# Cutting one long score product in two around a short one, in six of the twelve phases of an attention kernel

## The chip, the cores and the metric

The kernel runs on one core of one Trainium2 chip. The metric is the device time of one execution in microseconds. The kernel before took 1794.05 us (median of three runs, 1793.87 to 1794.19).

## What is computed

The input x has 32 images of 256 channels and 32 x 32 pixels, float32. With S = 1024 pixels (tokens), 8 heads of 32 channels, and a mask that lets a token see only tokens before it:

```python
xf = groupnorm(x, 32 groups).reshape(B, C, S)
q  = einsum('oc,bcs->bos', q_w,  xf) + q_b
kv = einsum('oc,bcs->bos', kv_w, xf) + kv_b        # k: first 256 rows, v: last 256
scores = einsum('bhqd,bhkd->bhqk', q, k) / sqrt(32)
scores = where(mask == 0, -10000, scores)
attn   = where(mask == 0, 0, softmax(scores))
out    = einsum('bhqk,bhkd->bhqd', attn, v)
return x + out.reshape(B, C, H, W)
```

All of it is float32. A float32 product on TensorE shows in the trace as two passes: two weight loads and two matmul records for each product of the program.

## The kernel before

**Batch, group, phase.** One image (a batch, b) is two groups of four heads (g), and each group is six phases (i = 0 to 5), so a batch is 12 phases and the whole run 384. The list VISITS (L583) says which blocks of the lower triangle of scores a phase computes. A phase has "longs" (up to 512 queries against one block of 128 keys) and "shorts": either a rectangle of 256 queries, or, in the phases 0, 1, 3 and 4, which PAIRS (L592) lists, the two blocks on the diagonal. `pair` (L291) lays such a pair out in 192 columns; for each half of the keys it takes one product of 128 columns and one of 64.

**Heads as row strips.** Head j has its 32 channels in the partitions 32j to 32j+31. One score product (`score`, L307) therefore uses 32 rows of TensorE's array, and with 64 keys 64 of its columns. Two heads with two halves of keys make four products of one size, which the program issues one after another. This document calls such four products a **wave**. The waves of heads 2 and 3 ("high") use the lower half of the array's rows, those of heads 0 and 1 ("low") the other half.

**PSUM.** A phase owns three PSUM tiles of two banks each: one for the longs of heads 0 and 1, one for the longs of heads 2 and 3, and one for the shorts of all four (L356). In the last of them a low head and a high head share a bank. The low shorts therefore wait on a semaphore, `bank_free`, which the last short of each high head and key half raises (L372 to L379).

**The order in a phase** is written out in `scores` (L348) and is the program's order on TensorE; the schedule is manual (L660), so nothing reorders it at build time. For a phase with one long and a pair (1, 3 and 4) it is:

1. high shorts: a wave of 128 columns, then one of 64
2. low long: a wave of 512
3. high long: a wave of 512
4. behind `bank_free`: low shorts, a wave of 128, then one of 64

Phase 0 has a pair and two longs (384 and 128 columns). There the list `begin` (L363) has two entries, and L364 to L365 take the high shorts in reverse (the wave of 64 first) with the 128-column low long between them. The function `scores_of` (L316) does that by its arguments `between` and `order`.

**After the scores**, ScalarE takes three exponentials from the three PSUM tiles (L391 to L397), GpSimd masks the diagonal blocks (L339), TensorE does one projection unit of the next batch (`pp` or `ppv`, L169), and then multiplies the exponentials of the phase before with the values (`acc`, L422). VectorE adds up keys (L440). DMAs fold the sums and move x, the inverses and the output; some of SP's DMAs are held back by `with_scores` (L511) until `bank_free` has reached a phase's count.

Of the kernel before, what the change touches and what calls it, by code (L numbers as in the profile page):

```python
# [26 lines left out]
HALFBANK = HALF // 2  # L27
# [5 lines left out]
def tile_norm_attention_residual(  # L33
# [65 lines left out]
    def unshifted():  # L99
# [207 lines left out]
        def score(b, g, bank, j, op):  # L307

            c, kb, first, width, cols = op
            rows = slice(HD * j, HD * (j + 1))  # L310
            return nc.tensor.matmul(  # L311
                bank[c : c + KEYS, cols], lhsT=live["k", b, g][rows, kb * P + c : kb * P + c + KEYS],
                rhs=live["q", b, g][rows, first : first + width], start=True, stop=True, skip_group_check=True,
            )

        def scores_of(b, g, bank_of, heads, entries, between=lambda: None, order=slice(None)):  # L316

            done = {}
            for _, _, halves in entries:
                for k, n in enumerate(list(range(max(map(len, halves))))[order]):  # L320
                    if k:
                        between()
                    for j in heads:
                        for c, ops in enumerate(halves):
                            if n < len(ops):
                                done.setdefault((j, c), []).append(score(b, g, bank_of(j), j, ops[n]))
            return done

        def mask(b, g, raw, j):


            hf, place = j // 2, (2 * j % 4) * P
            if ("e", b, g, "D", hf) not in live:
                live["e", b, g, "D", hf] = epool.tile(
                    [P, 4, HALF], F32, tag=("e0", "e")[hf], bufs=4, name=f"diagonal_{b}_{g}_{hf}"
                )
            square = live["e", b, g, "D", hf]
            for s in range(2):
                nc.gpsimd.affine_select(  # L339
                    out=square[:, :, place + s * P : place + (s + 1) * P],  # L340
                    in_=raw[:, :, (1 - s) * KEYS : (3 - s) * KEYS],
                    pattern=[[0, 4], [(1, -1)[s], P]], compare_op=ALU.is_gt, fill=0.0, base=0,
                    channel_multiplier=(-1, 1)[s],
                )
            if j == 0:
                nc.gpsimd.memset(square[0:1, :, 0:1], 1.0)

        def scores(b, v):  # L348


            g, i = divmod(v, len(VISITS))
            longs, shorts = VISITS[i]
            name = f"{b}_{g}_{i}"
            e = epool.tile([P, 4, HALF], F32, tag="e0" if i == TOTAL else "e", bufs=4, name=f"e_{name}")
            eh = epool.tile([P, 4, HALFBANK], F32, tag="eh", bufs=3, name=f"eh_{name}")
            pairs = [ps_s.tile([P, 2, HALF], F32, tag="sT", name=f"sT_{name}_{a}") for a in range(3)]  # L356
            short = pairs[2].rearrange("p bank (n q) -> p bank n q", n=2)
            short_of = lambda heads, *how: scores_of(
                b, g, lambda j: short[:, j % 2, j // 2, :], heads, shorts, *how
            )  # L360
            long_of = lambda heads, n: scores_of(b, g, lambda j: pairs[j // 2][:, j % 2, :], heads, longs[n : n + 1])
            rest = [lambda: long_of((2, 3), 1)] if len(longs) > 1 else []
            begin = [lambda n=n: long_of((0, 1), n) for n in range(len(longs) - 1, -1, -1)]  # L363
            if i in PAIRS and len(longs) > 1:  # L364
                first = short_of((2, 3), begin.pop(0), slice(None, None, -1))  # L365
            else:
                first = short_of((2, 3))
            for f in begin:
                f()
            long_of((2, 3), 0)  # L370

            ends = [made[-1] for made in first.values()]  # L372
            first = [ins for made in first.values() for ins in made]
            for ins in ends:
                ins.then_inc(bank_free, 1)
            for ins in first:
                tc.no_tile_sem_insts.add(ins.ins.name)
            live["free"] = live.get("free", 0) + len(ends)
            wait = nc.tensor.wait_ge(bank_free, live["free"])  # L379
            for ins in first:  # L380
                tc.declare_no_dep(wait.ins, ins.ins, reason="the semaphore orders them")
            made = short_of((0, 1), *rest if i in PAIRS else ())
            if i not in PAIRS:
                for f in rest:
                    f()
            for made in made.values():
                for lo in made:
                    for ins in first:
                        tc.declare_no_dep(lo.ins, ins.ins, reason="the semaphore orders them")
            wide, narrow = (max(at + width for at, width, _ in entries) for entries in (longs, shorts))  # L390
            for a in range(3):  # L391
                if a == 2:
                    exp = nc.scalar.activation(  # L393
                        eh.rearrange("p (n bank) q -> p bank n q", n=2)[:, :, :, :narrow], short[:, :, :, :narrow], AF.Exp
                    )
                else:
                    nc.scalar.activation(e[:, 2 * a : 2 * a + 2, :wide], pairs[a][:, :, :wide], AF.Exp)  # L397

            for ins in first:
                tc.add_to_no_dep_group(f"first_{name}", ins.ins)  # L400
                tc.add_to_no_dep_group("first", ins.ins)
            tc.declare_no_dep(exp.ins, group=f"first_{name}", reason="through the last two products")
            tc.declare_fence(exp.ins, group=f"first_{name}")
            live["e", b, g, "L", i], live["e", b, g, "H", i] = e, eh
            if i in PAIRS:
                mask(b, g, eh, PAIRS[i])

# [182 lines left out]
        ]  # L590
        N, TOTAL = NG * len(VISITS), 2
        PAIRS = {0: 0, 1: 1, 3: 3, 4: 2}  # L592

        PRODUCTS = [
            (0, [
# [36 lines left out]
        at, between, after = {}, {}, {}  # L632
# [27 lines left out]
        with tc.manual_schedule(engines={ENG.PE, ENG.Activation, ENG.DVE, ENG.Pool, ENG.SP}):  # L660
# [45 lines left out]
            for b in range(B):  # L706
                first, last = b * N, b == B - 1
# [3 lines left out]
                if b >= 2:  # L711
                    for n in range(NG * NH):
                        cols = slice(n % NH * HALF, (n % NH + 1) * HALF)
# [36 lines left out]
            for i in range(B * N + 1):  # L750
                if i < B * N:
                    scores(*divmod(i, N))
                for f in at.pop(i, ()):
                    f()
                b, v = divmod(i - 1, N)
                if i == B * N:

                    sums(3, SUMMED[v], False)
                if i:
                    values(b, v)  # L760
                    for f in between.pop(i, ()):
                        f()
                    if b < B - 1 or v not in SUMMED or v == 1:
                        add_keys(b, v)
                if i in (B * N - 2, B * N - 1):

                    sums(3, SUMMED[v])
                for f in after.pop(i, ()):
                    f()
# [9 lines left out]
    def shifted():  # L779


        with ExitStack() as inner:
# [34 lines left out]
            with tc.For_i(0, B, 1) as b:  # L817
# [93 lines left out]
                )  # L911

    inside = unshifted()
    ALL = 3 * P * ROW
    held = nc.values_load(
# [29 lines left out]
```

## Time and profile before

| what | value |
|---|---|
| median of three runs | 1794.05 us |
| the profiled execution's own time | 1793.44 us |
| its span in the trace | 1791.7 us |
| TensorE busy (matmuls) | 1784.4 us |
| VectorE / ScalarE / GpSimd busy | 1673.4 / 1456.4 / 881.3 us |
| granted TensorE clock | 0.999 |
| one batch, from a phase 0 to the next batch's phase 0 (from the second batch on) | 55.09 us |

How to read it: "PE" is TensorE's matmuls and "PEld" its weight loads. Matmul records overlap, because four row or column strips work side by side and because a record's end is modelled. A busy share near 100% therefore doesn't say that the array is full, and a mean duration of one record isn't the time by which it moves the end. What counts is where one record starts after another. All starts that are told below in ns are counted from the first weight load of the phase that they belong to.

### The profile page before, as it was taken

What the parts mean: (1) busy time and instruction counts of PE and PEld (TensorE: products, weight loads), DVE (VectorE), ACT (ScalarE), POOL (GpSimd) and SP (SyncE); (2) the same over time, 40 slices, a digit from 0 to 9 for tenths busy, and PEclk for the clock granted to TensorE, in tenths of its full rate; (3) what the DMA queues carried; (4) which work ended last, traced back from release to release, by engine and by line L of the source; (5) the groups of instructions that cost most, each with busy time, mean ns of one, the idle gap of its engine ahead of it and who ended that gap; (6) DMA issues with size and microseconds to landing.
All of it is one profiled execution on the core that took longest, in us unless ns stands there. A gap on an engine that the chain in (4) does not pass through costs nothing.

```text
span 1791.7 us, 81825 instructions
## 1 busy us (share of the span) xinstructions
PE 1784.4 (100%) x37036; PEld 948.2 (53%) x37036; DVE 1673.4 (93%) x1826; ACT 1456.4 (81%) x1990; POOL 881.3 (49%) x903
## 2 busy tenths in 40 slices
PE   9999999999999999999999999999999999999998
PEld 5555555555555555555555555555555555555554
DVE  4689999999999999999999999999999999999998
ACT  6888878888788888788887888878888878888785
POOL 2345544554545555445554455454555544555452
PEclk9999999999999999999999999999999999999999
DMA  2566766767667766766676676767776667666664
GB/s 70 105 115 137 134 134 129 147 135 143 127 126 149 140 138 134 135 139 138 139 135 131 129 150 132 145 125 128 149 141 135 136 134 138 139 139 137 132 107 106
DMA packets 86818, 236.77 MB, mean 132 GB/s; under 512 B 21312, under 2 KB 22336, under 8 KB 70592
## 3 DMA queue, kind: packets, MB, share of 16 engines
q0 software_dynamic: 15872, 97.53, 40.1%
q1 hardware_dynamic: 70448, 133.89, 25.5%
q8 instruction: 290, 4.75, 1.1%
q14 instruction: 64, 0.52, 0.1%
q10 hardware_dynamic: 144, 0.07, 0.0%
HBM read 66.85 MB, written 34.57 MB: 57 GB/s over the span
## 4 chain that ended last, share of the span: by engine, by line
PE 99%; ACT 0%; DVE 0%; issue 0%; POOL 0%; POOLq 0%
PE sT L311 31%; PE acc L422 28%; PE pp L169 26%; PE ppv L169 13%; PE pd L474 1%; PE busy L155 0%; ACT e L397 0%; PE pv L169 0%; PE pm L169 0%; PE wt L148 0%; DVE rb_last L547 0%; ACT eh L393 0%; DVE rb_last L534 0%; DVE turned L531 0%; DVE acc L544 0%
## 5 line engine op out<-in xcount | busy, mean ns | idle before, releaser
L339 POOL TENSOR_SCALAR_AFFINE_SELECT diagonal<-eh 128x512 f32<-128x512 f32 x512 | 632.5, 1256 | 841.5 <-ACT eh L393 840.9
L397 ACT ACTIVATE e<-sT 128x1024 f32<-128x1024 f32 x768 | 744.4, 1022 | 250.3 <-PE sT L311 225.9
L440 DVE TENSOR_TENSOR e<-e,e 128x1024 f32<-128x1024 f32 x314 | 574.2, 1829 | 24.5 <-ACT v L275 3.2
L311 PE MATMUL sT<-q,k 32*64 32x128 f32 (+2 forms) x18432 | 578.4, 372 | 0.1
L311 PEld LDWEIGHTS sT<-q,k 32*64 32x64 f32 x18432 | 394.8, 131 | 188.4 <-PE sT L311 69.6
L169 PE MATMUL pp<-xn,wT 128*32 128x512 f32 x4096 | 492.2, 598 | 0.0
L422 PE MATMUL acc<-e,v 128*32 128x512 f32 (+3 forms) x4608 | 401.0, 450 | 0.0
L393 ACT ACTIVATE eh<-sT 128x768 f32<-128x768 f32 (+1 forms) x384 | 341.7, 890 | 0.0
L422 PEld LDWEIGHTS acc<-e,v 128*32 128x32 f32 x4608 | 149.2, 110 | 261.5 <-issue 238.9
L169 PE MATMUL ppv<-wT,xn 128*32 128x256 f32 x4096 | 247.5, 382 | 0.0
L440 DVE TENSOR_TENSOR diagonal<-diagonal,e 128x1536 f32<-128x1536 f32 x126 | 195.0, 1548 | 16.8 <-PE acc L422 9.2
L169 PEld LDWEIGHTS pp<-xn,wT 128*32 128x32 f32 x4096 | 107.0, 109 | 195.7 <-issue 163.7
L440 DVE TENSOR_TENSOR e<-e,eh 128x1024 f32<-128x1024 f32 x126 | 164.2, 1303 | 6.5
L422 PEld LDWEIGHTS acc<-diagonal,v 128*32 128x32 f32 x4096 | 121.1, 110 | 87.6 <-issue 76.0
L440 DVE TENSOR_TENSOR e<-e,diagonal 128x2048 f32<-128x2048 f32 x63 | 144.2, 2289 | 19.8 <-POOL diagonal L339 19.8
L169 PEld LDWEIGHTS ppv<-wT,xn 128*32 128x32 f32 x4096 | 120.1, 109 | 79.7 <-issue 7.0
L422 PE MATMUL acc<-diagonal,v 128*32 128x128 f32 x4096 | 158.7, 273 | 0.0
L244 ACT ACTIVATE xn<-x,shift,rstd 128x256 f32<-128x256 f32 x248 | 136.8, 608 | 0.6 <-POOL shift L229 0.6
L544 DVE TENSOR_TENSOR num<-num,rb 128x512 f32<-128x512 f32 x124 | 123.3, 994 | 0.2 <-DMA rb<-inverses 0.2
L453 POOL DMA_DIRECT2D e<-e x124 | 103.3, 833 | 38.2 <-issue 38.2
L547 DVE SCALAR_TENSOR_TENSOR rb<-num,v_bias_col,x 128x256 f32<-128x256 f32 x248 | 117.5, 515 | 4.4
L453 POOL DMA_DIRECT2D diagonal<-diagonal x124 | 104.1, 839 | 4.8 <-issue 4.8
(84 smaller groups left out, 984.4 us busy)
## 6 DMA issues: line engine op xcount, KB each, us to landing
x<-in_x_dram SPq DMA_DIRECT2D x124, 256.0 KB, 3.7
diagonal<-diagonal POOLq DMA_DIRECT2D x62, 512.0 KB, 5.4
e<-e POOLq DMA_DIRECT2D x62, 512.0 KB, 5.9
rb<-inverses SPq DMA_DIRECT2D x124, 256.0 KB, 3.9
out_dram<-rb SPq DMA_DIRECT2D x124, 256.0 KB, 4.9
diagonal<-diagonal POOLq DMA_DIRECT2D x62, 256.0 KB, 4.6
folded<-diagonal SPq DMA_DIRECT2D x62, 256.0 KB, 5.1
e<-e POOLq DMA_DIRECT2D x62, 256.0 KB, 5.0
```

The lines of the kernel that those rows point to most:

```text
L169: nc.tensor.matmul(out[part], lhsT=lhsT[:, part], rhs=rhs, start=start, stop=stop, skip_group_check=True)
L244: nc.scalar.activation(to, of, AF.Identity, bias=live["shift", b][:, g : g + 1], scale=rstd)
L311: return nc.tensor.matmul(bank[c : c + KEYS, cols], lhsT=live["k", b, g][rows, kb * P + c : kb * P + c + KEYS], rhs=live["q", b, g][rows, ...
L339: nc.gpsimd.affine_select(out=square[:, :, place + s * P : place + (s + 1) * P], in_=raw[:, :, (1 - s) * KEYS : (3 - s) * KEYS], pattern=[ ...
L393: exp = nc.scalar.activation(eh.rearrange("p (n bank) q -> p bank n q", n=2)[:, :, :, :narrow], short[:, :, :, :narrow], AF.Exp)
L397: nc.scalar.activation(e[:, 2 * a : 2 * a + 2, :wide], pairs[a][:, :, :wide], AF.Exp)
L422: nc.tensor.matmul(acc[HD * j : HD * (j + 1), of], lhsT=live["v", b][:, kb, h * HD : (h + 1) * HD], rhs=e[:, j, :], start=first, stop=last ...
L440: nc.vector.tensor_add(to, to, tile_of(b, g, at))
L453: nc.gpsimd.dma_start(out=total[:rows], in_=total[rows : 2 * rows], accum_op=ALU.add)
L474: nc.tensor.matmul(pd[HD * j : HD * (j + 1), of], lhsT=pick, rhs=e[:, j, :], start=start, stop=stop, skip_group_check=True,)
L544: nc.vector.tensor_mul(num, num, rb)
L547: nc.vector.scalar_tensor_tensor(blocks(rb, s), blocks(num, s, (start + s) % 2 == 1), v_bias_col[:, g : g + 1], blocks(xt[:, g, cols], s), ...
```

## The change

In the phases 1, 3 and 4 of both groups (six of a batch's twelve) the low long, one wave of 512 columns, becomes two waves of 256 columns each, written to the two halves of the same banks. They are put around the high short of 128 columns, and the high short of 64 columns now comes first. All other phases stay as they are, and no other engine gets, loses or moves an instruction.

```diff
+        def part_of(b, g, bank, entry, n):
+
+            at, _, halves = entry
+            start = n * HALFBANK
+            for j in (0, 1):
+                for ((c, kb, first, _, cols),) in halves:
+                    score(b, g, bank[:, j, :], j, (
+                        c, kb, first + start, HALFBANK, slice(cols.start + start, cols.start + start + HALFBANK)
+                    ))
...
-            if i in PAIRS and len(longs) > 1:
+            if i in SPLIT:
+                begin = [lambda n=n: part_of(b, g, pairs[0], longs[0], n) for n in range(2)]
+            if i in PAIRS and len(begin) > 1:
                 first = short_of((2, 3), begin.pop(0), slice(None, None, -1))
             else:
                 first = short_of((2, 3))
...
         PAIRS = {0: 0, 1: 1, 3: 3, 4: 2}
+        SPLIT = 1, 3, 4
```

The order of these phases, before and after (H: heads 2 and 3, L: heads 0 and 1, with the columns of the wave):

```
before:  H128  H64   L512  H512  | bank_free |  L128  L64
after:   H64   L256  H128  L256  H512  | bank_free |  L128  L64
```

## Prediction

> **What bounds the kernel now.** I read the busy times and the chain of waits first, then the list of TensorE's waits, then groups by shape, then single phases.
>
> ```profile
> PE 1784.4 (100%) x37036; PEld 948.2 (53%) x37036; DVE 1673.4 (93%) x1826; ACT 1456.4 (81%) x1990; POOL 881.3 (49%) x903
> ...
> PE 99%; ACT 0%; DVE 0%; issue 0%; POOL 0%; POOLq 0%
> PE sT L311 31%; PE acc L422 28%; PE pp L169 26%; PE ppv L169 13%; PE pd L474 1%; PE busy L155 0%; ACT e L397 0%; PE pv L169 0%; PE pm L169 0%; PE wt L148 0%; DVE rb_last L547 0%; ACT eh L393 0%; DVE rb_last L534 0%; DVE turned L531 0%; DVE acc L544 0%
> ```
>
> The chain that ends last is TensorE's own stream, 99% of it, and the scores (sT) are 31%. VectorE's 93% does not set the end. The phase starts of one batch and the next lie 55.09 us apart, within 2 ns from the second batch on, so a saving inside a phase repeats 32 times.
>
> The groups by shape give the waves concerned:
>
> ```profile
> L311 PE MATMUL sT<-q,k 32*64 32x512 f32 x4096 | 359.4, 600 | 0.1
> L311 PE MATMUL sT<-q,k 32*64 32x128 f32 x6144 | 284.2, 278 | 0.0
> L311 PE MATMUL sT<-q,k 32*64 32x64 f32 x4096 | 155.8, 220 | 0.0
> ```
>
> The means (600 ns) include latency. What moves the end is the start-to-start distance of two passes on one row strip, read record by record: 429 ns for 512 columns, 216 for 256, 109 for 128, 56 for 64. The next view is the busy table over a phase 1, the one phase 4 with a longer time, and a phase 0; the first column is the phase from its first weight load to the first load of the work behind it.
>
> ```profile
> 904.77:906.18 1.40, 1.40 (x52) 1.06 (x48) 1.26 (x3) 0.78 (x2) 1.40 (x2) 1.00 0.10 18
> ...
> 918.55:919.97 1.41, 1.41 (x60) 1.07 (x48) 1.38 (x3) 0.37 (x2) 1.41 (x2) 1.00 0.00 0
> ...
> 927.79:929.21 1.42, 1.42 (x68) 1.16 (x64) 1.42 (x1) 1.25 (x3) 0.89 (x1) 1.00 0.51 188
> ```
>
> The phases 1, 3, 7, 9, 10 of a batch (7, 9 and 10 are 1, 3 and 4 of the second group) take 1403.6 ns, phase 4 takes 1410.9, phase 0 1419.3, all within a few ns in all batches.
>
> **Where those 1403.6 ns go.** Each half of the array has 704 columns to stream: two passes of 512, 128 and 64, or 2 x (429 + 109 + 56) = 1188 ns. High loads at 0, streams from 52 (as its second pass at 162 shows), and its 512 starts at 385 and 817: it is done at about 817 + 20 + 429. Low loads only at 53, streams from 106, and is never held up after that: 512 at 106 and 535, 128 at 964 and 1074, 64 at 1183 and 1239. The last of its four starts at 1259, and the next work's load comes 145 ns later, at 1404. So **low sets the end, and what it lost is the start**: 53 ns. Products are handed out 6.7 ns apart in program order; two high waves (8 x 6.7 = 53) stand ahead of it. In phase 0, 2 and 5 only one high wave stands ahead, and low loads at 27.
>
> **Two rules of the Trainium skill.** "TensorE: Matmul & The Clock Gate", in Part 3, "The mechanism", says that matmuls start in strict program order. The trace differs: in phase 5 the low wave's second pass starts at 188 and the earlier-issued high wave's second pass at 268. Order holds on a row strip, not across strips; I go by the trace, and so cutting low's long cannot hold high back by order alone. The same page (its table at the top) gives a queue of 64 entries with a partial reorder window. This the trace supports, sharply. In phase 0 (H64 L128 H128 L384 H384) the first of the H384 products loads at 280, when its strip is free, but the 2nd to 4th load at 357, 373 and 390. A product is four entries, so the 18th product of a phase is 17 x 4 = 68 entries behind the first. The first product's second pass starts at 108 and its record takes 217, so it ends at 325, and 31 ns later the 18th loads. The 30th product (L64) loads at 1133, and the 13th (L384) ends at 620 + 481 = 1101: 31 ns again. So a product is let in when the one 17 places ahead is finished, and then one per 17 ns. The delay shows in these ends, 17 ns apart, of the second pass of H384:
>
> ```profile
> 928.09 0.92 PE L311 MATMUL sT<-q,k 32*64 32x384 f32 x14
> 928.09 0.93 PE L311 MATMUL sT<-q,k 32*64 32x384 f32 x15
> 928.09 0.95 PE L311 MATMUL sT<-q,k 32*64 32x384 f32 x16
> ```
>
> I go by this rule for the forecast.
>
> **The change, part by part.**
>
> 1. *Four more products in each of 192 phases* (768 in all, 1536 weight loads and as many passes). Low streams four passes of 216 (864) in place of two of 429 (858): +6 ns a phase on low. The loads themselves lie under the other passes: each new pass of 216 ns hides a load that has to lead by 52.
> 2. *64 first, low second.* Low loads at 27, not 53: -26 ns. Its passes: 256 at 79, 295, 511, 727; 128 at 943 and 1052; 64 at 1161 and 1217, last of four 1237; next load 145 later, **1382**.
> 3. *The semaphore.* It is now raised by the 128, whose second pass starts at 278 to 298 and ends 267 later: 565. Before, the 64's ended at 347 + 217 = 564. The low shorts behind it load at 730 in phase 0 with the same end, and are due at 943. SP's held DMAs are released at the same time. No cost.
> 4. *What is queued behind:* H512 is now products 17 to 20. The first three waves stand as in phase 0 as far as timing goes (64 first, 128 third), so its loads come at 280, 357, 373, 390. A load leads its stream by 52, so the fourth one streams from 442, not 20 behind the first (387 + 20 = 407). Its second pass starts at 442 + 429 = 871. From the last second pass to the next load: 145 ns for 64 columns (56 + 89), 302 for 256 (216 + 86), so about 429 + 85 = 514 for 512. Next load at **1385 to 1386**.
>
> High is now the later by some 4 ns, and sets the end: **1386**. Gain 1403.6 - 1386 = 17.6 ns in five phases of a batch. In phase 4 of the first group the fourth product of L512, the 12th of the phase, loads 6 ns late (17 places behind the `acc` work, across the small `pm` product), which costs 7 ns to the end; the 12th product is now an H128, due only at 111, so this goes too: 1410.9 - 1386 = 24.9. A batch: 5 x 17.6 + 24.9 = 112.9 ns; 32 batches: 3.61 us. In the last batch two of the phases (2.05 and 2.63 us long) wait for ScalarE inside, and I give them nothing: -0.035. **Sum -3.58 us.** Against the profiled execution (1793.44, span 1791.7) that is a span of 1788.1; the median stands 0.6 us above that execution, so 1794.05 - 3.58 = **1790.5 us**.
>
> *ScalarE:* its first exponential waits for the low long: before, last pass at 555 + 588 = 1143; after, 747 + 374 = 1121, 22 ns earlier against a phase 18 shorter, so TensorE's later waits for exponentials keep their distance. The second exponential needs H512, at 871 + 587 = 1458 and not 1424, but the first one takes 1022, so it isn't due before 2140. VectorE has 3.9 us of idle time in a batch (7% of 55), and nothing is taken from it. All other engines' programs are the same in order and number.
>
> **Rivals.**
>
> - *No late loads (H512 comes all at once).* If the queue rule doesn't hold in this order, low ends the phase at 1382: 21.6 x 5 + 28.9 = 137 ns a batch, -4.35 us, **1789.7**. For it: the rule is read from one phase kind. Against: two exact hits of 31 ns. Chance 0.12.
> - *The gain is lost again.* Either the wave order brings low no earlier load, or H512 comes a little later than in phase 0; at 18 ns later the phase is back at 1404: **1794**. Chance 0.11 with all cases between this and the forecast.
> - *Slower: H512 is held behind the second L256.* It stands behind it in program order. If it could be let in only when that wave starts (511 in place of 280), it would stream from 563 to 583, its second pass would start at 1012, and the phase would end at 1526: +122 ns in 192 phases, +23.5 us, **1817.6**. It decides from a fourth load at 408, against 390. For it: everything behind a full queue waits in order. Against: in phase 0 H384 loads at 280 behind an L384 that starts at 298. Any lesser delay of this kind that costs over 3.6 us (19 ns a phase) is in this case's chance, 0.10.
> - The change does what it says: the instruction order of TensorE shows exactly the four waves moved, so no chance is kept for that rival.
>
> **How the numbers follow.** Forecast 0.67 at 1790.5 (its own width 1790.0 to 1791.1: 3 ns on each phase, mostly from the 514). A measurement of this kernel tells about 0.2% (3.59 us) from no change, and the forecast stands on that line. So its 0.67 splits in about equal parts; with the first rival faster is 0.45, with the second rival same is 0.45, slower 0.10. The range runs from just under the first rival, 1789.5, into the second, 1793.2, which leaves out some 0.17.
>
> **What would show it.** In the new trace: low's first load at 27; L256 at 79 (effective), 295, 511, 727; loads of H512 at 280, 357, 373, 390; last second pass of H512 at 871; phases of 1386 ns; a batch of 54.98 us; 768 more products. It is wrong if H512's loads come later than 390, if low's second L256 doesn't start at 511, or if the time between phases grows.

## The result and the profile after

The changed kernel takes 1802.22 us (median of 6 runs, 1801.38 to 1803.64) and the kernel before, on the same chip, 1794.01 us (1793.7 to 1794.19). The ratio is 1.0046, with a 95% interval of 1.0033 to 1.0059: slower by about 8.2 us, where 3.6 us less than before were forecast. The time is outside the range, and on the other side of the kernel before. (Of all the executions in this document one, of e7, had a granted clock of 0.65 and took 2580 us; it is left out of the ratios.)

Three lines of the page, after:

```profile
PE 1790.5 (99%) x38572; PEld 956.5 (53%) x38572; DVE 1668.6 (93%) x1826; ACT 1455.6 (81%) x1990; POOL 867.6 (48%) x903
...
q8 instruction: 302, 4.95, 1.1%
...
PE 99%; ACT 0%; issue 0%; DVE 0%; DMA 0%; POOLq 0%; POOL 0%; SPq 0%; ACTq 0%
```

The span is 1800.6 us and this execution's own time 1802.27. TensorE still sets the end (99%), and it has the 1536 matmuls more that were announced. Two things are new. "issue", a wait for nothing that the profile shows, has moved up in the chain. And queue 8, which carries the instructions themselves, moved 302 blocks. Before it moved fewer:

```profile
q8 instruction: 290, 4.75, 1.1%
```

The columns are packets, megabytes and the share of the DMA engines. 4.95 MB in 302 packets are 16 KB each, which fits 256 entries of 64 bytes, if a product is four entries (two loads, two matmuls): the 768 new products are then 3072 entries, and these are the 12 blocks more.

TensorE's own waits (total, times, longest) name the second surprise:

```profile
PE sT L311 <- issue: 1.4, 4, 0.6
PE pp L169 <- ACT e L409: 0.9, 1, 0.9
```

Neither line was there before. They count only the time in which no matmul record is open, and records overlap and end late, so the loss itself is larger (it is measured below). Of the groups by shape, the 512s lost 1536 of their 4096 records, and the 256s gained 3072:

```profile
L311 PE MATMUL sT<-q,k 32*64 32x256 f32 x5120 | 373.5, 387 | 0.3 <-ACT e L409 0.3
...
L311 PE MATMUL sT<-q,k 32*64 32x512 f32 x2560 | 302.1, 598 | 0.0
L311 PE MATMUL sT<-q,k 32*64 32x128 f32 x6144 | 282.2, 276 | 1.4 <-issue 1.4
```

The busy table over a phase 3, a phase 4 and the longest phase 10 (the same columns as in the prediction):

```profile
918.23:919.64 1.41, 1.41 (x60) 1.09 (x56) 1.38 (x4) 1.11 (x3) 0.00 (x0) 1.00 0.91 180
923.26:924.68 1.41, 1.41 (x68) 1.09 (x56) 1.38 (x3) 0.40 (x2) 1.41 (x2) 1.00 0.04 12
119.90:122.40 2.50, 1.94 (x60) 1.26 (x56) 2.39 (x3) 1.60 (x3) 1.24 (x2) 1.00 0.02 1
```

An ordinary changed phase takes 1411 to 1412 ns, forecast 1386. Some changed phases take far longer: this phase 10 takes 2.50 us, and TensorE has a record open for 1.94 of them.

**Where the 8 us are.** I took the times from one phase start to the next for the batches 1 to 30, the 10th percentile of each of the 12 steps as its clean time, and everything over 100 ns above as a **gap**. The sum of the 12 clean steps, the **clean batch**, is 55.130 us, before 55.087: +0.043 x 30 = 1.3 us. There are 13 gaps, in the phases 1, 7 and 10, of 7.3 us together. The sum, 8.6 us, is the difference of the two traces in these batches (8.61). Against the forecast (-0.113 us a batch, or 55.09 to 54.98) that makes two faults: 25 ns too much in every changed phase, and gaps.

**Fault one: the low shorts load late.** Up to the low shorts all starts of the waves stand where the prediction has them, to 1 ns: low loads at 27, the later L256 passes start at 295, 511, 727, H512 loads at 280, 357, 373, 390, and the last of its second passes starts at 872. The exception is the low shorts behind `bank_free`. First the weight loads of a phase 3 before (it starts at 913.53), then after (918.23); the brackets hold the idle time and who ended it:

```profile
914.26 0.50 PEld L311 LDWEIGHTS sT<-q,k 32*64 32x64 f32 x12 [0.19 <-PE sT L311]
```

```profile
919.15 0.29 PEld L311 LDWEIGHTS sT<-q,k 32*64 32x64 f32 x9 [0.26 <-PE sT L311]
```

They load at 727 before and at 920 after. The stream follows 53 later, at 973, and is due at 943: 30 ns late, and 1382 + 30 = 1412 is the phase. The signalling 128-column wave itself ends at 565, as forecast. But ahead of it in program order stands L256, on another row strip, and its last record ends at 315 + 374 = 689. The trace also records each raise of `bank_free`. Before, the four stand at 557, 600, 642 and 685; after, at 750, 792, 835 and 877. In both, the load follows the fourth by 42 to 43 ns. So it is the signal that is late, by 193 ns, and its first raise comes only after the end of L256. These times show one thing more: the four raises follow one another 42.5 ns apart, and these three distances are 128 of the 165 ns that the prediction's numbers have between the end of the signalling wave and the load.

**Fault two: TensorE has no instructions.** The longest phase 10 (it starts at 119.90), as the timeline shows it:

```profile
120.29 1.07 PE L311 MATMUL sT<-q,k 32*64 32x512 f32 x17
...
121.09 1.02 ACT L409 ACTIVATE e<-sT 128x1024 f32<-128x1024 f32 x1 [0.90 <-PE sT L311]
...
121.92 0.33 PE L311 MATMUL sT<-q,k 32*64 32x128 f32 x4 [0.56 <-issue]
121.92 0.20 PEld L311 LDWEIGHTS sT<-q,k 32*64 32x64 f32 x7 [0.91 <-issue]
```

The last raise of `bank_free` came 0.877 us into this phase, at 120.78, and yet TensorE starts nothing from 120.99 to 121.92. The transfer log has one 16 KB block on queue 8 that ended 0.63 us after this phase's start, at 120.53: 1.4 us ahead of the gap's end.

Two countings tie the gaps to the blocks. The first counts TensorE's entries in the trace from the first one on, in the order of their starts. The five longest pauses between two starts in the batches 1 to 30 (0.96 to 0.56 us) come just after 4801, 15041, 31169, 53441 and 62401 entries, and each of these numbers is 193 more than a multiple of 256. The pauses stand at one place of a block, though at different places of the program. The second compares times. Call *margin* the time from the end of a block's transfer to the moment when TensorE gets to the block's first entry. Before, the margin was 1.60 us at the least, and there are no gaps. After, the six longest pauses at a block's start (0.96 to 0.32 us) have margins of 0.46 to 1.06 us, and margin and pause add up to 1.36 to 1.47 us each time (the next, 1.34 and 0.28, fits less well). So in this trace **a block is usable about 1.4 us after its last byte, and TensorE pauses when the margin is less**. How much of a pause becomes a gap depends on what is still running: in e5 below, eight margins of 0.77 to 1.05 us delay TensorE's entries by 0.24 to 0.51 us, but cost a batch at most 0.12 us.

Where a transfer is called for can only be fitted: in this trace every transfer starts 1 to 5.6 us after the entry that stands 320 entries ahead of its block, and takes about 1 us (0.9 to 1.8).

The wait of `pp` that the profile puts down to the exponential `e` is one of these gaps (a pause of 0.96 us, margin 0.50, in phase 1 of batch 6). First the lines of that place, ScalarE's and TensorE's, then those of batch 7, without a gap:

```profile
356.71 1.94 ACT L409 ACTIVATE e<-sT 128x1024 f32<-128x1024 f32 x2 [0.46 <-PE sT L311]
```

```profile
357.89 1.06 PE L169 MATMUL pp<-xn,wT 128*32 128x512 f32 x8 [0.89 <-ACT e L409]
```

```profile
413.08 1.94 ACT L409 ACTIVATE e<-sT 128x1024 f32<-128x1024 f32 x2 [0.47 <-PE sT L311]
```

```profile
413.30 1.49 PE L169 MATMUL pp<-xn,wT 128*32 128x512 f32 x11
```

In batch 7 `pp` starts 0.22 us after the exponentials begin, so it doesn't wait for them. So where instructions are missing, the releaser that a profile infers can be one that had nothing to do with it.

Why now and not before? A batch before is 2306 entries, 9 x 256 + 2, so the blocks are called for at nearly the same places of every batch, which happen to be good ones (e6 to e8 test this). After, it is 2402 = 9 x 256 + 98, and the places wander over the whole batch.

### The profile page after: what moved, and what is told of

Same layout as the page of the kernel before. It is cut to its first block, busy times and chain, and to the rows that moved or that the text cites. A ratio compares the mean times of both kernels' runs of the same rounds, so it can differ in the third digit from the quotient of the medians.

```text
span 1800.6 us, 84897 instructions
## 1 busy us (share of the span) xinstructions
PE 1790.5 (99%) x38572; PEld 956.5 (53%) x38572; DVE 1668.6 (93%) x1826; ACT 1455.6 (81%) x1990; POOL 867.6 (48%) x903
## 3 DMA queue, kind: packets, MB, share of 16 engines
q8 instruction: 302, 4.95, 1.1%
## 4 chain that ended last, share of the span: by engine, by line
PE 99%; ACT 0%; issue 0%; DVE 0%; DMA 0%; POOLq 0%; POOL 0%; SPq 0%; ACTq 0%
PE sT L311 31%; PE acc L434 27%; PE pp L169 26%; PE ppv L169 13%; PE pd L486 1%; ACT e L409 0%; DMA x<-in_x_dram 0%; PE pv L169 0%; PE pm L169 0%; PE wt L148 0%; POOLq L682 0%; DVE rb_last L559 0%; ACT eh L405 0%; DVE rb_last L546 0%; PE busy L155 0%
## 5 line engine op out<-in xcount | busy, mean ns | idle before, releaser
L349 POOL TENSOR_SCALAR_AFFINE_SELECT diagonal<-eh 128x512 f32<-128x512 f32 x512 | 616.5, 1225 | 862.6 <-ACT eh L405 861.5
L311 PEld LDWEIGHTS sT<-q,k 32*64 32x64 f32 x19968 | 401.9, 131 | 186.9 <-PE sT L311 81.4
```

Of the source, the lines that this page charges most:

```text
L311: return nc.tensor.matmul(bank[c : c + KEYS, cols], lhsT=live["k", b, g][rows, kb * P + c : kb * P + c + KEYS], rhs=live["q", b, g][rows, ...
L349: nc.gpsimd.affine_select(out=square[:, :, place + s * P : place + (s + 1) * P], in_=raw[:, :, (1 - s) * KEYS : (3 - s) * KEYS], pattern=[ ...
```

## The experiments

All kernels compute the whole reference. The table gives medians, the ratio to the kernel before on the same chip, and the clean batch and the gaps of the batches 1 to 30. These last two columns are from the one profiled execution of each kernel, while the medians of the changed kernel and of e1 to e11 are over 4 to 20; in e9 and e10 the executions spread over 25 and 15 us.

| run | median us | ratio, 95% interval | clean batch us | gaps: count, us |
|---|---|---|---|---|
| before | 1793.52 to 1794.01 | | 55.087 | 0 |
| after | 1802.22 | 1.0046 (1.0033 to 1.0059) | 55.130 | 13, 7.3 |
| e1_cut128 | 1801.16 | 1.0038 (1.0026 to 1.0049) | 54.978 | 18, 10.9 |
| e2_whole | 1883.75 | 1.0506 (1.0488 to 1.0523) | 57.845 | 5, 2.5 |
| e3_pad_good | 1796.61 | 1.0017 (1.0011 to 1.0024) | 55.128 | 2, 0.2 |
| e4_pad_bad | 1847.05 | 1.0291 (1.0274 to 1.0309) | (most batches have one) | 48 over e3 |
| e5_cut_pad | 1792.28 | 0.9994 (0.9985 to 1.0002) | 54.979 | 3, 0.4 |
| e6_before_n64 | 1805.28 | 1.0062 (1.0048 to 1.0075) | 55.082 | 19, 10.6 |
| e7_before_n120 | 1794.46 | 1.0004 (0.9995 to 1.0012) | 55.085 | 1, 0.3 |
| e8_before_n184 | 1799.61 | 1.0032 (1.0021 to 1.0043) | 55.085 | 13, 7.4 |
| e9_cut_p41 | 1817.8 | 1.0128 (1.009 to 1.0166) | 54.984 | 18, 28.1 |
| e10_cut_p49 | 1814.11 | 1.0124 (1.0109 to 1.0139) | 54.985 | 23, 13.6 |
| e11_cut_p77 | 1792.35 | 0.9995 (0.9987 to 1.0003) | 54.978 | 6, 2.0 |

### The signal: e1 and e2

e1 cuts the low long as 128 + 384 columns, so that what stands ahead of the signalling wave ends early. e2 doesn't cut it: the order is H64, L512, H128, H512.

```diff
e1, in part_of:
-            start = n * HALFBANK
+            start, size = ((0, P), (P, HALF - P))[n]
...
e2, in scores:
-                begin = [lambda n=n: part_of(b, g, pairs[0], longs[0], n) for n in range(2)]
+                begin = [lambda: long_of((0, 1), 0), lambda: None]
```

> Edit: in the phases 1, 3 and 4 the low long is cut into 128 and 384 columns in place of 256 and 256; number and order of products stay as in the changed kernel. Theory: a matmul's semaphore is raised in program order, so the raise of H128 waits for the wave ahead of it, L256, which ends at 689 (and then 16 entries at 4.2 ns); with L128 ahead, which ends at 475, H128's own end at 565 counts again, the low shorts load at 730 in place of 920, and these phases take 1386 ns in place of 1412. The other loss, TensorE running out of instructions (some 7 us), hangs on the number of instructions and stays. Time 1797.3 us (1795.5 to 1799). Rival: the late load comes from the four added products in the queue, not from the size of the wave ahead: phases of 1412, 1802 us.

> Edit: the phases 1, 3 and 4 in the order H64 L512 H128 H512, with the low long uncut, so with as many products as before the change. Theory (raises in program order): H128's raise waits for L512, which ends at 508 + 20 + 587 = 1115, and 67 more; the low shorts load at about 1346 in place of 730 and stream from 1399 in place of 937, so these phases take about 1838 ns (before: 1404), 192 times 0.43 = +83 us: 1877 us. No stall for instructions. Rival (a product raises its semaphore at its own end): low starts 26 ns earlier and nothing is cut, phases of 1376, -5.5 us: 1788.5 us.

A phase 3 of e1 (it starts at 917.28), its window, and the loads behind `bank_free`:

```profile
917.28:918.67 1.39, 1.39 (x60) 1.09 (x57) 1.35 (x4) 1.09 (x3) 0.00 (x0) 1.00 0.90 177
```

```profile
918.01 0.37 PEld L311 LDWEIGHTS sT<-q,k 32*64 32x64 f32 x8 [0.15 <-PE sT L311]
```

The low shorts load at 730, as forecast, and all six phases take 1387 to 1388 ns: the forecast's number for the halves, once the signal is in time. The rest of the sum for a phase was right, then, and the rival (the four added products in the queue) is out, since e1 has them too. The whole run was outside what was expected for it (1797.3, at most 1799), since the gaps didn't stay but grew to 10.9 us.

A phase 3 of e2 (start 958.25):

```profile
958.25:960.12 1.86, 1.86 (x52) 0.97 (x48) 1.83 (x4) 1.57 (x3) 0.00 (x0) 1.00 0.54 149
```

```profile
959.62 0.42 PEld L311 LDWEIGHTS sT<-q,k 32*64 32x64 f32 x16 [0.83 <-PE sT L311]
```

The 128-column wave starts and ends in e2 as early as in e1 (its last record ends at 298 + 267 = 565), and yet the loads come at 1372. L512, ahead of it in program order, ends at 528 + 587 = 1115. The rival (a signal follows its own matmul) had 1376-ns phases and 1788.5 us; it is refuted by 95 us. The raises are recorded here too: at 560, 602, 645 and 687 in e1, and at 1202, 1245, 1287 and 1330 in e2. **A signal waits for the wave ahead of it in program order, although that wave runs on other row strips.**

My rule for what comes after that end, 4.2 ns for each of the 16 entries of the signalling wave (67 ns) and the 165 ns as before, fits the changed kernel (920 - 689 = 231) and is 26 ns short in e2 (1372 - 1115 = 257), which is the miss of e2's phase: 1864 ns for 1838. The raises say where the 26 ns are. From the end of the wave ahead to the first raise are 61 ns in the changed kernel and 87 in e2. In e2 the L512 wave ends with a raise of another semaphore, at 1160, and the first of `bank_free` follows 42 ns after it; in the changed kernel the first L256 has no such raise. So it seems that a raise which stands ahead takes a place in the row as well. What the 61 ns are made of stays open.

### The instructions: e3 and e4

Both are the changed kernel with no-operations (instructions that do nothing) on TensorE, ahead of the `acc` work. 158 of them in a batch bring it from 2402 to 2560 entries, ten whole blocks, so that the blocks are called for at the same places in every batch. The only difference between the two is the first batch: 57 no-operations in e3 and 229 in e4, which sets where these places are.

```diff
         def values(b, v):
             g, i = divmod(v, len(VISITS))
+            for _ in range(PADS[b == 0][v] if b < B - 1 else 0):
+                nc.tensor.nop(hint="pad", nofuse=True)
```

> Edit: the changed kernel with 158 no-operations on TensorE's queue in each batch but the last (13 or 14 ahead of the value products of a phase), so that a batch has 10 x 256 entries and the blocks of 256 in which instructions are fetched begin at the same places in every batch; fewer in the first batch (57), which sets these places away from the stretches where a fetch starts late. Theory: the ten or so long phases of the changed kernel (0.1 to 1.1 us over 1.41) are TensorE waiting for its next block of instructions; none is left, phases of 1412 stay: 1802.2 - 7.3 = 1794.9 us, and up to 1.5 us for the no-operations themselves. Rival (the long phases come from the order of the waves, or from ScalarE): as many long phases, 1802 us or more.

> Edit: as the run before, with the same number of no-operations per batch, but 229 in the first batch, which moves the places where blocks begin by 84 entries, into stretches where a fetch starts late. Theory: a wait for instructions in nearly every batch, at the same one or two phases, 0.3 to 0.9 us each: 9 to 25 us over the run before, 1804 to 1820 us. Rival: nothing but the no-operations in the first batch differs, so the time is that of the run before, within 1 us.

e3 lost the gaps, with 4810 instructions more, and a clean batch isn't longer for them (55.128). Its median of 1796.61 is 0.2 us above the upper end of what was expected (1796.4). e4, with 172 more than e3 in the first of 32 batches, takes 50.4 us more. Its waits of TensorE:

```profile
PE acc L436 <- issue: 33.2, 29, 2.2
PE sT L311 <- issue: 3.7, 5, 1.1
```

In e3 no line with "issue" stands among TensorE's waits. The direction was expected, the size was not: at the bad place the loss recurs in nearly every batch (the step from phase 9 to phase 10 has a median of 6.17 us in place of 5.00).

### Both taken away: e5

e5 is e1 with the no-operations of e3.

> Both costs found so far are taken away at once: the low long product is cut 128 + 384 columns, so the wave of heads 2, 3 whose signal releases the shorts stands behind products that end early (phases of 1387 ns, shown), and the no-operations on TensorE bring each batch to ten blocks of 256 queue entries, aligned as in the run that had no instruction gap. Theory (late signal and instruction supply are the two costs, and they add): phases 1387, batch 55.136 - 6 x 0.025 = 54.99 us, no gaps, 1796.6 - 192 x 0.025 = 1791.8 us (1790.5 to 1792.8), below the kernel before by about 0.1%. Rival (each no-operation costs a slot of its own, so the padding eats what the cut saves): 1794 or more. Rival (the shorter phases move the fetches into a crowded place again): gaps return, 1796 or more.

The two causes add up, as expected: 1792.28 is in the range, with phases of 1386 to 1387 ns, a batch of 54.979 us, hardly a gap. A phase 3:

```profile
912.39:913.78 1.39, 1.39 (x60) 1.09 (x56) 1.35 (x4) 1.09 (x3) 0.00 (x0) 1.00 0.89 171
```

The profiled execution has a span of 1789.0 us, 2.7 below that of before, but it is the fastest of 13 (1790.73 to 1794.99). The median is 1792.28, and the interval reaches from -0.15% to +0.02%: a gain of this size isn't resolved. By the two ratios (0.9994 and 1.0046, whose intervals lie apart) it is 0.5% faster than the changed kernel.

### The kernel before, moved: e6, e7, e8

If its alignment alone keeps the kernel before free of gaps, no-operations in its first batch alone must bring them. K no-operations move all blocks by K entries (64, 120 and 184), by the same edit as in e3 with a list for the first batch only.

> The kernel before, with 64 no-operations on TensorE in the first batch only. Its batches hold 9 x 256 + 2 queue entries, so the blocks in which instructions are fetched stand at the same places of all batches, and 64 entries move all of them. Theory (the kernel before is free of instruction gaps by its alignment only): blocks are now called for in phase 11 and at the start of phase 0, where transfers crowd, and come late by up to 0.2 us in some 14 places: +2.2 us at the least, perhaps several times that where a late block delays the next; 1796 to 1812. Rival (alignment plays no part; only the 64 entries cost, 4 ns each): 1793.5 to 1794.1.

> As the run with 64, but with 120 no-operations in the first batch, which puts the blocks between the crowded places. Theory: no gaps, the time of the kernel before within 0.6 us (1793.3 to 1794.6), although nearly twice as many no-operations are added. Rival (the no-operations themselves cost): more than with 64.

> As before, with 184 no-operations in the first batch: the blocks are called for in phase 8, where the fetches of the changed kernel came late. Theory: at least +2.3 us, and up to the 50 us that the badly aligned padding showed: 1796 to 1845. Rival (alignment plays no part): 1793.5 to 1794.6.

All three came as the theory has it: 1805.28, 1794.46 and 1799.61 us. 120 cost nothing that is resolved (0.9 us, and the interval holds 1), 64 cost 11.7 us, so the count doesn't matter and the position does. A gap of e6, in a phase 1:

```profile
1023.08 0.33 PE L311 MATMUL sT<-q,k 32*64 32x64 f32 x4 [1.38 <-issue]
1023.08 0.19 PEld L311 LDWEIGHTS sT<-q,k 32*64 32x64 f32 x3 [1.52 <-issue]
```

This is work that the change never touched: the kernel before loses 10.6 us in its 30 middle batches from 64 instructions that do nothing. Its six longest pauses again come at 193 entries over a multiple of 256.

### Looking for a better place: e9, e10, e11

The time of e5 spreads over 4 us, and its smallest margins were 0.77 to 1.05 us, in the `acc` work of phase 4. Three runs have 41, 49 and 77 no-operations in the first batch in place of 57, and so move the blocks by 16, 8 and 20 entries. (With fewer no-operations a block is called for later in the program's work, not earlier as the first expectation says.)

```diff
-        PADS = (13, 14, ...), (6, 6, 5, 5, 5, 5, 5, 5, 5, 5, 5, 13)
+        PADS = (13, 14, ...), (4, 4, 4, 4, 4, 4, 4, 4, 3, 3, 3, 13)      # e9
```

> The cut 128 + 384 with padding as in the run with 57, but 41 no-operations in the first batch, so that every block is called for 16 entries earlier. In the run with 57 the smallest margins between a block's arrival and its need were 0.77 to 1.05 us, in phase 4, and its times spread from 1790.7 to 1795.0. Theory (that spread is blocks that come late in some executions): from the arrivals of all runs the smallest margin is now 2.6 us; time 1790.7 to 1791.5 with a spread under 1.5 us, so about 0.13% under the kernel before. Rival (the spread has another source, as the transfers of data): 1792.3 with the same spread.

> As the run with 41, with 49 in the first batch. Theory: smallest margin 2.6 us; 1790.7 to 1791.5, narrow spread. Rival: 1792.3, wide spread.

> As the run with 41, with 77 in the first batch, on the other side of 57. Theory: smallest margin 2.3 us; 1790.7 to 1791.8, narrow spread. Rival: 1792.3, wide spread.

Two are clear misses. e9 and e10 lose 28.1 and 13.6 us in gaps; TensorE's waits in e9:

```profile
PE ppv L169 <- issue: 11.0, 8, 2.1
PE acc L436 <- issue: 2.5, 8, 0.3
```

In e9 one block per batch is called for 26 or 27 ns after the start of phase 2 (by the fit of 320 entries). In 22 of the 30 batches its transfer began 1.7 to 3.1 us later, and in the other eight, batch 14 among them, only after 5.9 to 6.8 us. Earlier traces had called for blocks within 0.1 us of the same point, eight times in e7 and twice each in e8, e1 and the changed kernel, and every one of these transfers began within 2.4 us. So arrivals in one run don't foretell those in another, not even at the same place; that e3 and e5 met a good place was in part luck. e11 is as good as e5 and no better, with its spread, and that spread is not explained. (e5 ran on another chip than e9 to e11; the kernel before takes 1793.5 us on both, and e11 agrees with e5.)

**What is shown and what is argued.** Shown: the position of the blocks in the program makes or removes gaps (e3 against e4, and e6 to e8 against before), the long pauses stand where a block begins, and they end about 1.4 us after a transfer on queue 8. Argued only: that a transfer on queue 8 starts late because data transfers stand ahead of it. No run took the data transfers away, and the traces don't settle it: over the blocks of one trace, the delay of the transfer goes with the bytes that queue 0 moves around the call (from 0.5 us ahead of it to 1.5 us behind) in before, the changed kernel and e6 (correlations of 0.39, 0.36 and 0.53), but not in e9 (-0.14). So which positions are good can't be told in advance.

## Why the prediction was wrong

- *What bounds the kernel*: right. TensorE's stream sets the end, and a phase repeats 32 times.
- *Step 1, four more products*: right for what the array streams, and the second step that failed. It missed that 768 products are also 3072 entries that have to be fetched, and so put that cost at nothing without a reason. "The loads themselves lie under the other passes" was the only cost looked at. The runs show gaps of 7.3 us in its place.
- *Step 2, low loads at 27 and not 53*: right, every pass of the low long to 1 ns. The low shorts at 943 and the end at 1382 came true only once the signal was in time (e1 and e5).
- *Step 3, the semaphore*: this is the first step that failed. "It is now raised by the 128, whose second pass starts at 278 to 298 and ends 267 later: 565", and from it "No cost". The wave ends there, but its signal stood behind L256, and its first raise is at 750; the load is at 920, not 730. Two things were missing, and neither alone would have cost anything. The release counts from the end of L256, 689, and not from 565: with the old 165 ns the load would come at 854 and the stream start at 907, where it is due at 943. And from that end to the load are not 165 but 231 ns. I took the 165 ns from phases in which no longer wave stood ahead of the signalling one, and didn't say that the trace doesn't show the other case. The prediction had weighed the Trainium skill's sentence on program order ("TensorE: Matmul & The Clock Gate", Part 3, "The mechanism") for starts alone; the page says it of ends too. The runs split it: starts keep their order only within a row strip, and the modelled ends of the records don't keep it either (565 ahead of 689), but signals keep it across strips (e1, e2). The price: 25 to 26 ns in each of 192 phases against the forecast, 0.0255 x 192 = 4.9 us.
- *Step 4, H512 behind the full queue*: right, all four loads to the nanosecond. The rule read from the queue of 64 entries holds in these phases. With step 3's fault removed (e1, e5) the phase is 1387, where "1385 to 1386" stood.
- *Phase 4's extra 7 ns*: right, it is gone (1412 like the others, and 1387 in e1).
- *ScalarE and the other engines*: right in that no engine but TensorE sets the end. The one wait for an exponential that is new (0.9 us) is a gap in the instructions, as shown above.
- *The sum*: 1790.5 + 4.9 (signal) + 7.3 (gaps) = 1802.7, measured 1802.2. The second term appears nowhere in the prediction: the line of queue 8 stood on the page of before and wasn't read. The Trainium skill has a section on it ("Runtime: NRT & Kernel Launch", "Instruction fetch mechanics"): blocks of 16 KiB with 256 instructions, at a cost that is mostly hidden. The size of a block agrees with the 302 packets. "Mostly hidden" fits the kernel before, which has no gap, and doesn't hold for the others: single waits for instructions reach 2.2 us (e4).
- *Rivals and chances*: slower had 0.10, and all of it rested on a delay of H512. The delay that came was one wave further on, at the low shorts, and low's end comes 30 ns late for it (1412 for 1382). The range stopped at the case in which the gain is lost; it had no term for a signal behind a longer product, and none for instructions.

## What to carry to other kernels

When a product that raises a semaphore is moved behind a longer one, count its signal from the end of that longer product, not from its own, even if both run on different strips of the array, and add a distance for each raise (42.5 ns here). If the last product of the wave alone raised the semaphore, an estimate from these distances has the load at 920 - 128 = 792 in the changed kernel, which is in time; no run tests it. When a change adds instructions to an engine that has no idle time, look at the instruction queue as well: count the entries of a loop body modulo the block, and test the position with a few no-operations ahead of the loop before a difference of half a per cent is put down to the edit itself. An edit can be right by its own phase, as the cut of 128 + 384 is (1387 ns for 1404), and lose by alignment more than it gains, as e1 does.

## What the hardware showed beyond that

- No-operations on TensorE, 158 in a batch, cost no measurable time in a clean batch of this stream: 55.128 us with, 55.130 without.
- A shift of 8 to 16 entries (0.5 to 1 KB of instructions) took the same kernel from 1792.28 to 1814.11 and 1817.8 us (e5, e10, e9), while one of 20 in the other direction left it at 1792.35 (e11).
- The fetch of a block began 1 to 5.6 us after the place that allowed it in the changed kernel, and up to 6.8 us in e9, if the place is the entry 320 ahead of the block; its transfer took about 1 us.
